# Spreading the twelve gates over the partitions: from TensorE and ScalarE to the DMA queue of GpSimd

## The chip, the core and the metric

One NeuronCore of a Trainium2 chip runs the whole program in one launch. The metric is the device time in microseconds (us), the median of three runs. Engine names are those of the profile: PE is TensorE's matrix multiplication, PEld its weight loads, DVE is VectorE, ACT is ScalarE, POOL is GpSimd, SP the engine that issues most of the DMAs. A name with a q (SPq, POOLq) is the engine's own instruction queue.

## The reference, cut to what matters

Four sequences (b) of 1024 rows and 256 columns go through a transformer block and then through a second cross attention. In the block, nine modulation vectors of 256 numbers are computed for each sequence, and three of them are **gates**: they multiply what the self attention, the cross attention and the MLP give back before it is added to x.

```
m = silu(mod) @ w_ada + b_ada                      # per sequence: 9 x 256
sh_msa, sc_msa, g_msa, sh_mca, sc_mca, g_mca, sh_mlp, sc_mlp, g_mlp = ...
h = _self_attn(_ln(x) * (1 + sc_msa) + sh_msa, w_qkv, b_qkv, w_so, b_so)
x = x + h * g_msa
h = _topk_cross_attn(..., w_co, b_co);   x = x + h * g_mca
h = _swiglu(..., w_m1, b_m1, w_m2, b_m2); x = x + h * g_mlp
# then the second cross attention, without gates
```

Each of the three branches ends in a product with a weight and the addition of a bias row, so h * g is the same as a product with a weight whose columns were multiplied by the gate, plus a bias row multiplied by the gate. That is how the kernel applies gates: it multiplies w_so, w_co and w_m2, and the rows b_so, b_co and b_m2, once for each of the four sequences.

## The kernel before, in words

Rows are worked on in 16 units of 256 rows (b = sequence, part = quarter of it). Every unit goes through five stages: self attention, selection (the sixteen largest of 77 scores), cross attention, MLP and last attention. All is float32, apart from a few small tiles.

**Order.** Nothing runs in the order in which the source is written. Every operation is handed to a planner (`Plan`, line 222) with an engine, an expected cost, buffers and a priority. `place` (line 311) simulates the engines with these costs, picks buffers from rings, and makes one list; `issue` (line 368) then calls the operations' functions in that list's order. An engine executes its own instructions strictly in that order, and semaphores do the rest. So a function that issues no instruction still takes its place, its cost and its buffers in the plan.

**Gates.** `mod_gate(i)` (line 721, three calls, each for all four sequences) multiplies the activated condition with a chunk of w_ada on PE (line 727) and adds the bias on DVE (line 730); the result is `gates`, a tile of 4 partitions (one for each sequence) by 3 by 256. For the multiplication a gate is needed on all 128 partitions. `gated(b)` (line 1292) does that for sequence b and each of its three gates, called here g0 to g11 with number 3b + i:

- PE, line 1303: a product of a column of the identity, repeated over 128 columns, with the gate's row; this puts the row on all partitions of one of the two PSUM banks of the ring `mm`.
- ACT, line 1306: copies it from PSUM to a tile `gate` of 128 x 256. There are two such tiles (line 861), used in turn.
- POOL, line 1308: bias row times gate; and POOL, line 1310: weight times gate. After both, the `gate` tile is free again.

The weight and the row come by DMAs from SP (`load`, line 589). By the order of times in the trace the two `gate` tiles serve g0, g2, g4, g6, g7, g8 and g1, g3, g5, g9, g10, g11: g5 is held until its weight w_m2 is multiplied late.

**Names used later.** L755: ACT writes the modulated context, out of PSUM. L970 and L973: transposes of small tiles on PE and their copy on ACT. L1098, L1104: the second pass of self attention scores on PE, both needed by the exponential L1108 on ACT; L1116: its weighted sum. L1075: values, L938: projections with a 256 x 256 weight, L1035: output projections, L1247 and L1275: the MLP, L1212: weighted sums of cross attention, all on PE. L919: transposes of the normalized rows. L902, L905, L912: statistics and normalization on DVE, with L907 and L909 (POOL) in their middle. L996: the maximum over scores on DVE. L1011 and L1023: the additions and products of the softmax normalization on POOL. L1049: POOL adds a bias row to x. L1079: DVE adds the values' bias. L1335: idle products that keep PE active. On POOL all these share one queue with L1308 and L1310.

Two buffers decide much of PE's order: `mm` has two PSUM banks, and the scores' `s` has one.

Of the kernel before, what the change touches and what calls it, by code (L numbers as in the profile page):

```python
# [9 lines left out]
F32 = mybir.dt.float32  # L10
BF16 = mybir.dt.bfloat16
AF = mybir.ActivationFunctionType
ALU = mybir.AluOpType
# [3 lines left out]
P = 128  # L17
# [371 lines left out]
def tile_block(ctx: ExitStack, tc: tile.TileContext, a: dict, out: bass.AP):  # L389
    nc = tc.nc  # L390

    x_d, cond_d, ctx_d = a["x"], a["cond_1024"], a["ctx_1024"]
    B, L, C = x_d.shape
# [16 lines left out]
    def ctile(shape, name, dt=F32):  # L410
        return const.tile(shape, dt, tag=name, name=name)
# [7 lines left out]
    ident = ctile([P, P], "ident")  # L419
# [25 lines left out]
    for i in range(3):  # L445
        t = ctile([P, TU, 4, 32], f"parts{i}", BF16)
# [5 lines left out]
    for i in range(2):  # L452
        t = ctile([P, TU, H // 2, VP], f"v_self{i}")
# [3 lines left out]
    pl = Plan()  # L457


    def f_pe(cols, n):  # L460
        return n * (cols * 0.00175 + 0.0095) + 0.1

    def f_act(n):
        return 0.21 + 0.00081 * n

    def f_dve(n):
        return 0.155 + 0.00104 * n

    def f_pool(n):
        return 0.13 + 0.00222 * n  # L470
# [7 lines left out]
    T_GATE = ("D", "D", 0.22, 0.05, 0.37, 0.216)  # L478
# [11 lines left out]
    def fixed(name, shape, dt=F32):  # L490
        return pl.fixed(ctile(shape, name, dt), name)
# [8 lines left out]
    n_mod = 26  # L500
    mod = fixed("mod", [P, n_mod, B])
    gates = fixed("gates", [B, 3, C])
    k_ctx = [fixed(f"k_{i}", [P, KC, B, 2, LC]) for i in range(2)]
    v_ctx = [fixed(f"v_{i}", [LC, B, H // 2, VP]) for i in range(2)]
    for v, fill in zip(v_ctx, (0.0, 1.0)):
# [7 lines left out]
    start, total = {}, 0  # L513
# [52 lines left out]
    bg_ada = at.buf("bg_ada", [B, 3, C])  # L566
# [22 lines left out]
    def load(buf, src, kb, prio, key=None, eng="SP", view=None):  # L589
        def fn():  # L590
            dst = buf() if view is None else view(buf())
            (nc.sync if eng == "SP" else nc.scalar).dma_start(dst, src)
        pl.op(eng, f_dma(kb) if eng == "SP" else 0.3, fn, w=[buf if key is None else (buf, key)],
              prio=prio, lag=2.0)
# [21 lines left out]
    for g, names in enumerate(groups):  # L616
        for name, hi in names:
            n, r = hi // P, n_rows[g]
# [11 lines left out]
    def chunk(name, lo, n, prio):  # L630
        c = pl.buf("chunk", f"{name}{lo}")
        load(c, a[name].rearrange("(kc p) n -> p kc n", p=P)[:, :, lo : lo + n], n, prio,
             view=lambda t: t[:, :, :n])
        early.append((chunk_lo, chunk_hi, c))
        return c
# [49 lines left out]
        nc.scalar.preload_act_table_set("natural_log_exp_and_others")  # L685
    pl.op("ACT", 1.5, silu, w=[sc_t], r=[pc], prio=-50, lag=-1.28)

    turn = [0]

    def mod_group(name, lo, m, scale_first, prio, dma_prio):  # L690
# [30 lines left out]
    def mod_gate(i, prio, dma_prio):  # L721
        c = chunk("L0_xcond_w_ada", (3 * i + 2) * C, C, dma_prio)
        pp = pl.buf("mm", f"modg{i}")

        def fn():
            for kc in range(KC):
                nc.tensor.matmul(pp()[:B, :C], sc_t()[:, kc, :B], c()[:, kc, :C],
                                 start=(kc == 0), stop=(kc == KC - 1))
        pl.op("PE", f_pe(C, 2), fn, w=[pp], r=[sc_t, c], prio=prio)
        pl.op("DVE", f_dve(256), lambda: nc.vector.tensor_tensor(  # L730
            gates()[:, i, :], pp()[:B, :C], bg_ada()[:, i, :], ALU.add), w=[(gates, i)], r=[pp, (bg_ada, i)], prio=prio)

    def filled(v):

# [55 lines left out]
    for i, key in enumerate("kqv"):  # L790
        weight(w_qkv, "L0_xcond_w_qkv", -84 + i, (1, 0, 2)[i] * C, C, key)
    mod_gate(0, -30, -79)
    mod_group("L0_xcond_w_ada", 3 * C, 6, False, -3, -70)
    load(cx, ctx_d.rearrange("b k c -> k b c"), 308, -69)
    weight(w_kv[0], "L0_xcond_w_kv", -68)
    weight(w_q0, "L0_xcond_w_q", -67)
    mod_gate(1, -2, -59)
    mod_group("L0_xcond_w_ada", 6 * C, 12, False, -1, -50)
    mod_gate(2, -1, -49)
    mod_group("L1_xcond_Wss_q", 0, 18, True, -1, -48)  # L800
    mod_group("L1_xcond_Wss_kv", 0, 22, True, -1, -47)
# [9 lines left out]
    for b in range(B):  # L811
        pl.op("DVE", 0.42, lambda b=b: nc.vector.bn_stats(st_c()[:LC, b, :], cx()[:, b, :]),
              w=[(st_c, b)], r=[cx], prio=-1)
    for b in range(B):
        pl.op("DVE", 0.16, lambda b=b: nc.vector.bn_aggr(mv_c()[:LC, b, :], st_c()[:LC, b, :]),
              w=[(mv_c, b)], r=[(st_c, b)], prio=-1)
# [475 lines left out]
    def gated(b, pr):  # L1292

        gw = {}
        for i, (key, name, kc) in enumerate(
            (("so", "L0_xcond_w_so", KC), ("co", "L0_xcond_w_co", KC), ("m2", "L0_xcond_w_m2", NF))
        ):
            first = None if b else DMA_FIRST[i]
            w, row = pl.buf("w_" + key, f"w_{key}{b}"), pl.buf("row", f"b_{key}{b}")
            gate, pg = pl.buf("gate", f"gate{b}{i}"), pl.buf("mm", f"pg{b}{i}")  # L1300
            load(w, a[name].rearrange("(kc p) n -> p kc n", p=P), 128 * kc, first or pr)
            load(row, a[f"L0_xcond_b_{key}"].partition_broadcast(P), 128, first or pr)
            pl.op("PE:gate", T_GATE, lambda i=i, pg=pg: nc.tensor.matmul(
                pg()[:, :C], ident[:B, b : b + 1].to_broadcast([B, P]), gates()[:, i, :], start=True, stop=True),
                w=[pg], r=[(gates, i)], prio=pr, take=[gate])
            pl.op("ACT:gate", f_act(256), lambda gate=gate, pg=pg: nc.scalar.copy(gate(), pg()[:, :C]),
                  w=[gate], r=[pg], prio=pr)
            pl.op("POOL:gate", f_pool(256), lambda row=row, gate=gate: nc.gpsimd.tensor_tensor(  # L1308
                row(), row(), gate(), ALU.mult), w=[row], r=[row, gate], prio=pr)
            pl.op("POOL:gate", f_pool(256 * kc), lambda w=w, gate=gate, kc=kc: nc.gpsimd.tensor_tensor(  # L1310
                w(), w(), gate().unsqueeze(1).to_broadcast([P, kc, C]), ALU.mult),
                w=[w], r=[w, gate], prio=pr)
            gw["b_" + key], gw["w_" + key] = row, w
        return gw

    stages = (self_attention, selection, cross_attention, mlp, last_attention)
    for b in range(B):
        pl.at = None
        gw = gated(b, b * NU - 0.5)
        for part in range(NU):  # L1320
            u = Unit()
            u.b, u.part, u.name = b, part, f"_{b}{part}"
            u.prio = float(b * NU + part)
            pl.at = None
            u.x = pl.buf("x", "x" + u.name)
            move_x(u, x_d, False)
            for k, stage in enumerate(stages):
                pl.at = (b * NU + part, k)
                u.prio = ORDER[b * NU + part][k]
                stage(u, gw)  # L1330
# [45 lines left out]
```

## Time and profile before

| | us |
|---|---|
| runs of the kernel (three) | 1040.08, 1040.41, 1044.87 |
| median | 1040.41 |
| the profiled execution | 1041.43 |
| its span, first to last instruction | 1039.4 |
| one core's granted TensorE clock, mean | 0.993 |

The profiled execution's time is 2.0 us more than its span, and 1.0 us more than the median of the runs. The page shows busy times of engines over the span, forty slices of it, the chain of work that ended last (followed back from the end by what released each instruction), and groups of instructions. For forty slices of 26 us:

```profile
PE   7899999999999999999999999999999999999997
...
DVE  5177999979899999947833446599999977724232
ACT  3358786687687794758468667877688765764665
POOL 3384445466353573557635647546335464753653
PEclk9799999999999999999999999999999999999999
DMA  7710000001000000100000200000000001000000
```

A digit is the busy share of a slice in tenths. DMA is busy only in the first two slices. The clock row's 7 is the one stretch with a lower granted clock, from 35.1 to 48.8 us of the span, where it was 0.5. PE is at 9 nearly everywhere, but busy includes waits between overlapping instructions.

### The profile page before, as it was taken

The page shows a single profiled execution, that of the slowest core. Times are in us where ns is not written, and L with a number is a line of the kernel's source. Part 1 is how long each engine was busy: PE and PEld are TensorE (multiplying, and loading weights), DVE is VectorE, ACT ScalarE, POOL GpSimd, SP SyncE. Part 2 cuts the span into 40 slices and gives each one's busy share as a digit, 9 for nine tenths or more (in the row PEclk, how much of TensorE's full clock was granted, in tenths as well). Part 3 has the DMA queues.
Part 4 walks back from the last instruction along what each step waited for, and adds up shares of the span by engine and source line. Part 5 has one row for each costly group of instructions (what it writes and reads, how often), then busy time and mean ns, then how long its engine had stood idle before and what let it go on. Part 6 is the DMA issues. An engine that isn't in the chain of part 4 may idle for free.

```text
span 1039.4 us, 27476 instructions
## 1 busy us (share of the span) xinstructions
PE 1012.0 (97%) x10363; PEld 770.5 (74%) x10363; DVE 757.3 (73%) x4000; ACT 723.5 (70%) x1270; POOL 542.1 (52%) x751
## 2 busy tenths in 40 slices
PE   7899999999999999999999999999999999999997
PEld 5667777777777778777877777778767787778775
DVE  5177999979899999947833446599999977724232
ACT  3358786687687794758468667877688765764665
POOL 3384445466353573557635647546335464753653
PEclk9799999999999999999999999999999999999999
DMA  7710000001000000100000200000000001000000
GB/s 255 242 50 7 3 2 1 3 3 36 3 22 27 7 3 5 38 16 22 21 1 2 82 22 21 2 2 2 2 2 22 2 2 42 12 1 12 2 21 21
DMA packets 23623, 27.01 MB, mean 26 GB/s; under 512 B 1609, under 2 KB 20675, under 8 KB 23491
## 3 DMA queue, kind: packets, MB, share of 16 engines
q1 hardware_dynamic: 23455, 25.26, 7.7%
q8 instruction: 81, 1.33, 0.5%
q14 instruction: 52, 0.42, 0.1%
q10 hardware_dynamic: 35, 0.01, 0.0%
HBM read 21.07 MB, written 4.19 MB: 24 GB/s over the span
## 4 chain that ended last, share of the span: by engine, by line
PE 48%; DVE 13%; ACT 6%; POOL 2%; issue 1%; POOLq 0%; ACTq 0%; DVEq 0%
PE mm L1247 13%; PE mm L1275 8%; PE mm L938 5%; PE mm L1035 5%; PE s L1196 4%; PE o L1212 3%; PE s L985 3%; DVE share L1153 2%; DVE r L1147 2%; DVE nm L996 2%; PE s L1186 1%; DVE share L1145 1%; DVE share L1151 1%; PE mm L919 1%; ACT prob L1108 1%
## 5 line engine op out<-in xcount | busy, mean ns | idle before, releaser
L1247 PE MATMUL mm<-share,w_m 128*128 128x256 f32 x640 | 150.3, 386 | 0.4 <-ACT share L926 0.2
L1205 ACT ACTIVATE prob<-s 77x2048 f32<-77x2048 f32 x64 | 120.0, 1875 | 43.7 <-PE s L1201 43.4
L996 DVE TENSOR_REDUCE nm<-s 128x16 f32<-128x2048 f32 (+1 forms) x64 | 119.0, 1859 | 38.0 <-PE s L985 17.2
L1247 PEld LDWEIGHTS mm<-share,w_m 128*128 128x128 f32 x640 | 117.7, 190 | 26.0 <-issue 4.7
L1147 DVE MATCH_REPLACE8 r<-share 128x77 f32<-128x77 f32 x512 | 109.9, 222 | 0.0
L1145 DVE MAX8 share<-share 128x8 f32<-128x77 f32 x512 | 94.4, 225 | 21.0 <-ACT share L1138 21.0
L1153 DVE MATCH_REPLACE8 share<-share,r 128x77 f32<-128x77 f32 x512 | 109.6, 221 | 0.0
L1011 POOL TENSOR_TENSOR share<-share 128x256 f32<-128x256 f32 x64 | 47.1, 736 | 96.4 <-ACT share L1008 95.1
L1151 DVE MAX8 share<-r 128x8 f32<-128x77 f32 x512 | 93.9, 224 | 0.0
L1247 PE MATMUL mm<-slab,w_m 128*128 128x256 f32 x384 | 92.9, 388 | 0.7 <-ACT slab L926 0.5
L1023 POOL TENSOR_TENSOR slab<-slab,share 128x256 f32<-128x256 f32 x96 | 69.4, 730 | 28.4 <-ACT share L1018 19.2
L1261 POOL TENSOR_SCALAR slab<-slab 128x512 f32<-128x512 f32 x43 | 64.4, 1498 | 36.8 <-ACT slab L1259 33.0
L1247 PEld LDWEIGHTS mm<-slab,w_m 128*128 128x128 f32 x384 | 69.9, 190 | 15.6 <-issue 3.1
L1275 PE MATMUL mm<-share,slab 128*128 128x256 f32 x344 | 80.9, 381 | 0.0
L1008 ACT ACTIVATE share<-o,mask 128x256 f32<-128x256 f32 x128 | 66.6, 575 | 12.2 <-PE o L1212 9.6
L1108 ACT ACTIVATE prob<-s 128x2048 f32<-128x2048 f32 x32 | 60.5, 1889 | 17.9 <-PE s L1104 17.5
L1044 DVE TENSOR_TENSOR slab<-slab,mm 128x512 f32<-128x512 f32 x52 | 35.4, 680 | 50.9 <-PE mm L1035 25.7
L1275 PEld LDWEIGHTS mm<-share,slab 128*128 128x128 f32 x344 | 64.7, 190 | 10.0 <-issue 0.9
L1253 ACT ACTIVATE slab<-mm,cols 128x256 f32<-128x256 f32 x90 | 43.0, 480 | 41.0 <-PE mm L1247 40.5
L1212 PE MATMUL o<-prob,v 77*32 77x256 f32 x1024 | 67.9, 385 | 0.8 <-ACT share L1018 0.5
L1049 POOL TENSOR_TENSOR slab<-slab,row 128x512 f32<-128x512 f32 x39 | 49.9, 1278 | 28.5 <-DVE slab L912 15.4
L907 POOL TENSOR_SCALAR rs<-mv 128x2 f32<-128x2 f32 x64 | 14.2, 222 | 81.7 <-DVE mv L905 78.8
(183 smaller groups left out, 2427.0 us busy)
## 6 DMA issues: line engine op xcount, KB each, us to landing
share<-in_L_xcond_w_m_dram SPq DMA_DIRECT2D x4, 1024.0 KB
slab<-in_x_dram SPq DMA_DIRECT2D x9, 256.0 KB, 2.9
out_dram<-slab SPq DMA_DIRECT2D x9, 256.0 KB, 2.7
w_m<-in_L_xcond_w_m_dram SPq DMA_DIRECT2D x4, 512.0 KB, 6.8
share<-in_L_xcond_w_ada_dram SPq DMA_DIRECT2D x3, 512.0 KB, 3.8
w_so<-in_L_xcond_w_so_dram SPq DMA_DIRECT2D x4, 256.0 KB
w_co<-in_L_xcond_w_co_dram SPq DMA_DIRECT2D x4, 256.0 KB, 4.0
w_qkv<-in_L_xcond_w_qkv_dram SPq DMA_DIRECT2D x3, 256.0 KB
```

Source lines behind the costliest of these rows:

```text
L996: pl.op("DVE:max", f_dve(n), lambda: nc.vector.tensor_reduce(nm()[:, t], s4(), AX.X, ALU.max, negate=True), w=[(nm, t)], r=[s], prio=u.prio)
L1008: pl.op("ACT:nln", 0.5, lambda e=e, own=own, other=other: nc.scalar.activation(nz()[:, e, :], o()[:, ts(e, UT)], AF.Ln, bias=own, scale=ot ...
L1023: nc.gpsimd.tensor_tensor(dst, dst, shaped(nz()[:, k, :], dst), op)
L1108: pl.op("ACT:exp", f_act(2048), lambda s=s, prob=prob: nc.scalar.activation(prob(), s(), AF.Exp), w=[prob], r=[s], prio=pr)
L1145: nc.vector.max(top()[:, h + i, 0:8], sc()[:, h + i])
L1147: nc.vector.match_replace(r1()[:, i], top()[:, h + i, 0:8], sc()[:, h + i], NEG)
L1151: nc.vector.max(top()[:, h + i, 8:16], r1()[:, i])
L1153: nc.vector.match_replace(sc()[:, h + i], top()[:, h + i, 8:16], r1()[:, i], NEG)
L1205: pl.op("ACT:exp", f_act(2048), lambda s=s, prob=prob: nc.scalar.activation(prob()[:LC], s()[:LC], AF.Exp), w=[prob], r=[s], prio=pr)
L1212: nc.tensor.matmul(o()[r, :UT] if drops is not None else o()[r, ts(e, UT)], columns(v_z()[:, b], 8 * c + 2 * j + e), prob()[:LC, j, ts(e, ...
L1247: nc.tensor.matmul(pp()[:, ts(half, UT)], w_m1()[:, kc, m : m + P], ht()[:, kc, :], start=(kc == 0), stop=(kc == KC - 1))
L1275: nc.tensor.matmul(pp()[:, ts(t, C)], gts[f // 2]()[:, f % 2, ts(t, P)], w_m2()[:, f, :], start=(f == 0), stop=(f == NF - 1))
```

## The change

A tensor `gates_d[i]` of 4 x 256 in the outer memory is added for each of the three gate kinds.

- In `mod_gate`, after the DVE addition, POOL's queue stores the finished `gates` row block to `gates_d[i]`; for the first two kinds the same function at once issues the read of the first gate into its tile (g0 and g1).
- `read_gate(n, place)` finds the next gate from number n on that uses the tile `place`, and issues, on POOL's queue, a DMA that reads its 256 numbers from the outer memory into all 128 partitions (1 KB to each, 128 KB written).
- In `gated`, PE's product and ACT's copy issue nothing any more, but they keep their place, cost and PSUM bank in the plan, so all other operations keep their order and their buffers.
- POOL's two multiplications stay. After the second of them, whichever comes second, `read_gate` is called for the next gate of the same tile.

```diff
+    dram = ctx.enter_context(tc.tile_pool(name="dram", bufs=1, space=bass.MemoryType.DRAM))
+    gates_d = [dram.tile([B, C], F32, tag=f"gates_d{i}", name=f"gates_d{i}") for i in range(3)]
...
+    gate_of = {}
+
+    def read_gate(n, place):
+        todo = [m for m in range(n, 3 * B) if gate_of[m]() is place]
+        if todo:
+            b, i = divmod(todo[0], 3)
+            nc.gpsimd.dma_start(place, gates_d[i][b, :].partition_broadcast(P))
...
-        pl.op("DVE", f_dve(256), lambda: nc.vector.tensor_tensor(
-            gates()[:, i, :], pp()[:B, :C], bg_ada()[:, i, :], ALU.add), w=[(gates, i)], r=[pp, (bg_ada, i)], prio=prio)
+        def add():
+            nc.vector.tensor_tensor(gates()[:, i, :], pp()[:B, :C], bg_ada()[:, i, :], ALU.add)
+            nc.gpsimd.dma_start(gates_d[i], gates()[:, i, :])
+            if i < 2:
+                read_gate(i, gate_of[i]())
+        pl.op("DVE", f_dve(256), add, w=[(gates, i)], r=[pp, (bg_ada, i)], prio=prio)
...
-            pl.op("PE:gate", T_GATE, lambda i=i, pg=pg: nc.tensor.matmul(
-                pg()[:, :C], ident[:B, b : b + 1].to_broadcast([B, P]), gates()[:, i, :], start=True, stop=True),
-                w=[pg], r=[(gates, i)], prio=pr, take=[gate])
-            pl.op("ACT:gate", f_act(256), lambda gate=gate, pg=pg: nc.scalar.copy(gate(), pg()[:, :C]),
-                  w=[gate], r=[pg], prio=pr)
+            gate_of[3 * b + i] = gate
+            pl.op("PE:gate", T_GATE, lambda: None, w=[pg], r=[(gates, i)], prio=pr, take=[gate])
+            pl.op("ACT:gate", f_act(256), lambda: None, w=[gate], r=[pg], prio=pr)
+            uses = []
+
+            def times_gate(t, g, n=3 * b + i, gate=gate, uses=uses):
+                nc.gpsimd.tensor_tensor(t, t, g, ALU.mult)
+                uses.append(t)
+                if len(uses) == 2:
+                    read_gate(n + 1, gate())
```

The two POOL operations of a gate then call `times_gate` with the row and with the weight, in place of the two multiplications written out there before.

## The prediction

> **What bounds the kernel now.** I read the busy shares first, then the chain of work that ended last, then, by windows, the chain and the timeline around each of the twelve gates.
>
> ```profile
> PE 1012.0 (97%) x10363; PEld 770.5 (74%) x10363; DVE 757.3 (73%) x4000; ACT 723.5 (70%) x1270; POOL 542.1 (52%) x751
> PE 48%; DVE 13%; ACT 6%; POOL 2%; issue 1%; POOLq 0%; ACTq 0%; DVEq 0%
> ```
>
> PE looks full, but carries only 48% of the span on the chain. The shares add up to about 70% because the chain can be followed back only to about 310 us. From there it runs on DVE up to 341 us, on PE for most of the rest, on DVE again about 500 to 514 us, and on POOL and ACT about 542 to 565 us. Before 310 us I use the busy times: DVE is busy 57.5 of 60 us in 120 to 180 and 55.9 in 240 to 300, so DVE nearly fills that stage too. A PE step is worth its time only where PE is on the chain.
>
> **What goes, and its price.** The sources of the three steps:
>
> ```profile
> L1303 PE MATMUL mm<-gates,ident x24: 372/454/791, 34.5 to 563.7; 4*128 4x256 f32 x24
> L1306 ACT COPY gate<-mm x12: 354/372/530, 35.2 to 567.4; 128x256 f32<-128x256 f32 x12
>   ACT gate L1306: 22.4, 6
> ```
>
> Twelve gates make 24 matmul records and 12 ACT copies of 0.37 us. The last line is of L1308, POOL's row product: POOL stood idle 22.4 us, six times, until a copy. That looks like the prize, but nothing is listed as waiting for L1308 or L1310, so it is idle time of an engine that is seldom the bound. In the stream a gate takes 0.52 to 0.63 us of PE, from its start to the next group's (336.08 to 336.61 for g8, 563.40 to 564.02 for g11). The copies save 12 x 0.37 = 4.5 us of ACT, which has 30% idle.
>
> **The start, to 60 us.** The half clock is granted here, and PE is what the others wait for (DVE waits 12.7 us for L1075).
>
> ```profile
> 37.28 1.22 PE L1303 MATMUL mm<-gates,ident 4*128 4x256 f32 x2 [0.89 <-ACT share L755]
> ...
> 38.97 0.81 PE L1098 MATMUL s<-slab,k_eo 32*128 32x128 f32 x6
> ...
> 42.11 1.16 PE L1303 MATMUL mm<-gates,ident 4*128 4x256 f32 x2
> 43.20 1.22 PE L1075 MATMUL mm<-w_qkv,slab 128*128 128x256 f32 x2
> ```
>
> g3 holds PE from 42.11 to 43.20: 1.09 us. g2 runs mixed into L1098: from L1098's first start to that of L1104 it is 2.45 us, against 1.87 for the next such pair at the same clock (46.91 to 48.78): 0.58. L755, whose last part frees the bank for L970, starts at 35.89 behind g0's slot and copy; without them about 0.5 earlier. Gain before L1075: 1.09 + 0.58 + 0.5 = **2.2 us**.
>
> Against it stand the new transfers. g0 to g3 are read before 60 us, 4 x 128 KB = 0.52 MB, in a stage where DMA moves 302 GB/s (36 to 48 us, share 0.90): loads behind them land up to 1.7 us later, and the last x loads land at 58.3. Their end is not the only thing waited for, so I take half: +0.9; bounds 0 and 1.7.
>
> The stores and first reads stand in POOL's queue between L909 (ends 8.3) and L821 (20.7), and between L965 (ends 24.1) and g0's product (35.6): holes of 12.4 and 11.5 us. In the second, POOL waits for the addition of gate 1 (ends 29.8), then for its store to land, then for gate 2's addition (31.4). A store of x lands 1.9 to 3.2 us after its issue in this trace; under load a 128 KB row took 6.7. Two issues plus 3 us from 29.8 reach about 35, still no later than 35.6; with 6.7 us, g0's product comes 3 us late, and the 4.56 us for which POOL is idle before L1011 (52.09) swallow that. If all this cover were gone, it would cost those 3 us.
>
> **What a POOL-issued DMA costs.** No row of before shows one. Nearest below is SP's issue of the same shape (a 128 KB row at 69.17): 0.35 us of its queue. The Trainium skill, "DMA: Bandwidth & Descriptors", Specifications, gives about 1 us to the first byte on the GpSimd path against about 0.6 on the SP path. But a rule speaks against the change: "SBUF — State Buffer", section "SBUF: two separate sides", says that GpSimd cannot write a DMA's descriptors while DVE holds their shared port pair, with 620 ns growing to 3100. DVE is busy 96% where g4 to g8 fall, though mostly in operations with two inputs or reductions, while the rule is about copies and operations with a scalar; the nearest candidate, L912, lasts 0.4 us. No run here shows the lock. By the first the price p of an issue is 1.0 us, by the second 3.1. I take **p = 1.0** with ends 0.35 and 3.1. Landing: SP's row of 69.17 had its packets moved by about 71.2, so 2 us.
>
> **Where p lands on the path.** Ten reads follow a second product; the page's question is what stands next on POOL. The tight one is behind g3's weight:
>
> ```profile
> 58.11 1.28 POOL L1310 TENSOR_TENSOR w_so<-w_so,gate 128x512 f32<-128x512 f32 x1
> ...
> 59.34 3.02 POOL L1023 TENSOR_TENSOR slab<-slab,share 128x256 f32<-128x256 f32 x4
> ...
> 62.75 0.71 POOL L909 TENSOR_TENSOR rs<-rs,mhalf 128x2 f32<-128x2 f32 x1
> 63.50 0.73 DVE L912 TENSOR_SCALAR slab<-slab,mv,rs 128x256 f32<-128x256 f32 x2 [0.77 <-POOL rs L909]
> ```
>
> POOL runs without a break from 55.4 into these, and DVE then sits idle 0.77 us for L909: +1.0. The start's sum is −2.2 + 0.9 + 1.0 = **−0.3**.
>
> In the DVE stage, 60 to 341 us, the PE slots of g4 to g8 (5 x 0.58 = 2.9) count nothing, since DVE is late next; bounds −2.9 and 0. Reads: behind 96.62 there is a chain of two operations, with idle 0.22 and then 1.78, so nothing at p = 1; behind 237.87 idle is 0.55, so +0.45, halved to +0.2 since L1049 there is followed by ACT work that is not DVE's. Behind g7 (335.23) g8 is read and needed at once: 1.0 + 2.0 us to land, 0.72 for the product, 338.95, where L961 now starts at 338.93: 0. That is the only place where the round trip replaces a PE and ACT path of the same length. The 2.59 us that POOL waited at 118.71 and the 6.26 at 107.77 go; what follows waits for DVE. Sum **+0.2**.
>
> After 341 us, the chain decides:
>
> ```profile
> 507.62 1.37 DVE nm L996
> ...
> 526.87 1.00 PE o L1212 x16
> 527.88 0.62 PE mm L1303 x2
> 528.50 0.59 PE mm L919 x4
> ...
> 562.76 1.76 ACT prob L1205
> ```
>
> g9 (507.29) lies beside DVE's maximum, g11 (563.40) beside ACT's exponential; g10 is itself a link, and 0.62 us go. Of 4.5 us of copies none is a link. Reads behind 424.32 (6.45 us idle), 510.43 (0.29, then 4.02) and 532.83 (1.49, and 8.49 of gate wait gone before it) are hidden; a price of 1 us without that cover would be 3 us. Sum **−0.6**.
>
> Total: −0.3 + 0.2 − 0.6 = −0.7 us. The profiled 1041.43 becomes 1040.7; that execution is 1.0 above the median of the runs, so on the runs' scale **1039.7**.
>
> **Rivals.**
> 1. *Every freed PE step counts* (PE is 97% busy, and the longer links are all PE's): 2.2 at the start and 8 x 0.58 = 4.6 in the stream, POOL's issues and the transfers hidden: −6.8, so 1033.6. Against it: DVE is on the chain or nearly full beside six of the eight.
> 2. *POOL becomes the late one* (slower). With p = 3: 3.0 behind g3's weight, 2.45 behind 237.87, 3 − 2.0 = 1.0 behind 96.62, 2.1 at g8; 8.5, less 2.2 − 0.9 and 0.6 of gains, +6.6: 1047. It decides from p of about 2.6, where four costs less the gains pass 5.2 us. For it: the descriptor rule and a DVE at 96%; against: the DVE operations there are mostly not the kind it names.
> 3. *The start slips.* All 1.7 us of transfer count, POOL's store wait too, and the clock, granted 0.5 for 13.65 us after PE's light stretch at 32 to 34 us, comes back later, since PE has still less to do at 34.5: each 3 us more of it cost about 1.5. Together +3: 1043.4.
> A fourth, that the gates aren't prefetched at all, is excluded but for g8: the other tiles come free many us ahead of use (g10: 510.4 against 530.9).
>
> **How the numbers follow.** Chances: forecast 0.50, first rival 0.17, second 0.23, third 0.10. What can be told from no change is 0.5%, 5.2 us: below 1035.2 or above 1045.6. Faster is the first rival, 0.17; slower the second and a third of the third's tail, 0.26; the rest 0.57. The range takes in most of both rivals: 1034 to 1047. The likeliest case alone, with 0 to 1.7 for the transfers and p from 0.35 to 1.5, is 1037.5 to 1041.5.
>
> **What would show it.** L1303 and L1306 are gone from the profile; L1075's first start is about 41 instead of 43.20; POOL shows 15 DMA issues, whose length is p; DVE's wait for L909 at 63 us is not under 0.77; in the chain L1212 is followed directly by L919 near 527. The forecast is wrong if an issue takes over 2.6 us, if DVE's instructions near the reads become longer, if the half-clock stretch changes in length, or if PE's freed slots in 60 to 341 us appear as an earlier end of that stage.

## The result, and the profile after

The changed kernel takes 1046.52 us in the median (1045.70 to 1048.57) against 1040.41 (1039.27 to 1044.87), nine runs of each. The ratio is 1.0057, interval 1.0044 to 1.007: 0.57% slower, just beyond the 0.5% that the forecast took for what can be told from no change. Its profiled execution took 1046.52 us with a span of 1044.6: 5.1 us more than the span before. In two experiments below (the first four gates by PE; the small DMA) the profiled execution has a spell of half clock between 289 and 298 us, worth 3.2 us, that no other trace here has; these two are read only up to 285 us.

The rows of the page that answer to those shown of before (busy time; the clock over forty slices; the chain that ended last), with the row of the new DMAs (size, median us from issue to landing):

```profile
PE 1004.2 (96%) x10339; PEld 766.0 (73%) x10339; DVE 759.9 (73%) x4000; ACT 720.1 (69%) x1258; POOL 552.6 (53%) x766
...
PEclk9889999999999999999999999999999999999999
...
PE 58%; DVE 24%; ACT 8%; POOL 5%; issue 2%; DMA 2%; POOLq 0%; ACTq 0%; DVEq 0%
...
gate<-gates_d POOLq DMA_DIRECT2D x12, 128.0 KB, 3.3
```

The removal did what it says: 24 matmul records and 12 copies are gone, PE is busy 7.8 us less and ACT 3.4. POOL has 15 instructions and 10.5 us more. The chain now has DMA in it, which before it had not.

**Where the time went** is found with one comparison: each DVE instruction of one trace is put beside the same instruction of the other, and its **lag** is how much later it starts, counted from each span's start. All lags in this document are against the profiled execution of the kernel before. In the changed kernel the lag is 0 up to 36 us, −3.4 at 47, +2.9 from 66 to 240, +5.0 at 300, +4.2 at 320, +5.9 from 380 to 500, and +5.1 from 545 to the end. So the terms are: the start **+2.9**, a jump at 243 us **+2.2**, a chance gain of −0.8 at 303 (a DVE subtraction that before met POOL there and took 1.49 us does not meet it now), a step at 343 us **+1.7**, and a gain at 500 to 530 us **−0.85**; the sum is the 5.1. (Line numbers have moved: L1308 and L1310 are both L1328 now, L912 is L930, L909 is L927, L1011 is L1029, L1023 is L1041, L1049 is L1067, L1158 is L1176, L1075 is L1093, L1212 is L1230, L919 is L937. L746 is a store, L699 a read. L785 and L798 are PE's products for the keys and the values of the context, L801 is DVE's addition behind the latter. In the kernels of the experiments the numbers differ by up to four from these, or from those of before.)

*The start.* Before, the product with w_m2 and L1011 stood so on POOL (start, us, what, and in brackets the idle time before it and what ended it):

```profile
42.34 4.51 POOL L1310 TENSOR_TENSOR share<-share,gate 128x2048 f32<-128x2048 f32 x1 [0.18 <-DMA share<-in_L_xcond_w_m_dram]
...
52.09 0.73 POOL L1011 TENSOR_TENSOR share<-share 128x256 f32<-128x256 f32 x1 [4.56 <-ACT share L1008]
```

In the changed kernel POOL's part of the timeline is this:

```profile
35.41 0.58 POOL L699 DMA_DIRECT2D gate<-gates_d  x1 [4.66 <-DMA gates_d<-gates]
35.98 0.53 POOL L746 DMA_DIRECT2D gates_d<-gates  x1
36.52 0.74 POOL L1328 TENSOR_TENSOR row<-row,gate 128x256 f32<-128x256 f32 x1
37.21 1.27 POOL L1328 TENSOR_TENSOR w_so<-w_so,gate 128x512 f32<-128x512 f32 x1
42.67 0.60 POOL L699 DMA_DIRECT2D gate<-gates_d  x1 [4.19 <-DMA gates_d<-gates]
...
48.70 4.53 POOL L1328 TENSOR_TENSOR share<-share,gate 128x2048 f32<-128x2048 f32 x1 [1.27 <-PE mm L785]
53.20 0.72 POOL L1328 TENSOR_TENSOR row<-row,gate 128x256 f32<-128x256 f32 x1
...
54.81 0.74 POOL L1029 TENSOR_TENSOR share<-share 128x256 f32<-128x256 f32 x1
```

Read it as a queue. The addition of gate kind 2 was done at 31.4, but its store stands behind the read of g1, which waits until 35.4 for store 1 to land (issued at 30.16); so store 2 leaves at 35.98, lands at 42.14, and the read of g2 stands before g1's products until then. That read lands at 48.58, so the product with w_m2 (42.34 before) starts at 48.70; the releaser named in its bracket is not the last one. L1029 comes at 54.81 instead of 52.09. The end of that chain, in windows (busy us of each engine, then granted clock, DMA share, GB/s), and DVE's and PE's instructions:

```profile
51.00:54.00 3.00, 0.99 (x5) 0.41 (x3) 0.00 (x0) 1.14 (x4) 2.91 (x2) 1.00 0.85 269
54.00:57.00 3.00, 0.00 (x0) 0.00 (x0) 0.29 (x1) 0.42 (x1) 2.60 (x5) 0.86 0.57 147
57.00:60.00 3.00, 1.78 (x7) 1.43 (x8) 2.90 (x11) 1.04 (x3) 2.44 (x4) 0.50 0.01 3
60.00:63.00 3.00, 3.00 (x9) 2.25 (x8) 0.89 (x4) 0.40 (x1) 2.60 (x4) 0.51 0.05 14
```

```profile
56.71 1.13 DVE L930 TENSOR_SCALAR slab<-slab,mv,rs 128x256 f32<-128x256 f32 x2 [5.93 <-POOL rs L927]
```

```profile
58.22 1.11 PE L937 MATMUL mm<-ident,slab 128*128 128x128 f32 x4 [6.23 <-DVE v L801]
```

PE has nothing to do from 52 to 58 us, since DVE waits 5.93 us for a small operation in POOL's queue. What doesn't need POOL still ran 4.2 us ahead of the kernel before up to there; the lag of this normalization is +1.8. And then the clock is half from about 56.1 to 63: a second half-clock stretch that the kernel before doesn't have. The first one became shorter, from about 35.7 to 42.5 us instead of from 35.1 to 48.8. The length of the second stretch does not decide the lag: it is 6.8 us in this trace and in those of "g7's read by SP" and "g8 by PE" below, which lag 2.9, 3.0 and 2.2 us at 80 us, and 3.4 us in "g7 by PE" and "small first reads", which lag 3.0 and 2.5.

*243 us.* POOL, and then the one DVE instruction that runs beside it:

```profile
241.00 0.65 POOL L699 DMA_DIRECT2D gate<-gates_d  x1 [0.30 <-POOL w_so L1328]
241.68 1.28 POOL L1067 TENSOR_TENSOR slab<-slab,row 128x512 f32<-128x512 f32 x1
242.92 0.72 POOL L1041 TENSOR_TENSOR slab<-slab,share 128x256 f32<-128x256 f32 x1
243.61 0.72 POOL L1029 TENSOR_TENSOR share<-share 128x256 f32<-128x256 f32 x1
...
245.67 0.72 POOL L1041 TENSOR_TENSOR slab<-slab,share 128x256 f32<-128x256 f32 x1
```

```profile
243.08 3.59 DVE L1176 TENSOR_TENSOR share<-share 128x256 f32<-128x256 f32 x1
```

A subtraction that takes 0.416 us in the median of its 32 took 3.59: it ends when POOL's fifth operation in a row ends, not after the first. Before, it took 0.41:

```profile
240.26 0.41 DVE L1158 TENSOR_TENSOR share<-share 128x256 f32<-128x256 f32 x1
```

*343 us.* The read of g8 and the first product that needs it:

```profile
340.41 0.66 POOL L699 DMA_DIRECT2D gate<-gates_d  x1 [0.30 <-POOL w_co L1328]
343.77 0.72 POOL L1328 TENSOR_TENSOR row<-row,gate 128x256 f32<-128x256 f32 x1 [2.71 <-DMA gate<-gates_d]
344.45 0.20 POOL L979 CAST parts<-nm 128x32 bf16<-128x32 f32 x1
```

The cast that follows (L961 before, at 338.93) came 0.96 us after the row's product then; now it stands directly behind it, 5.5 us later than before.

*500 to 530 us.* The gain is made at 509 us, on DVE. Before, a normalization beside g9 met POOL's weight product (POOL had waited 1.60 us for the copy of g9), and the pair took 1.69 us; it stands in the chain that ended last. Now the product comes ahead of it, and the pair takes 0.84. Before, then after:

```profile
508.90 1.69 DVE L912 TENSOR_SCALAR share<-slab,mv,rs 128x256 f32<-128x256 f32 x2
509.06 1.37 POOL L1310 TENSOR_TENSOR w_so<-w_so,gate 128x512 f32<-128x512 f32 x1
```

```profile
513.37 1.27 POOL L1328 TENSOR_TENSOR w_so<-w_so,gate 128x512 f32<-128x512 f32 x1
514.84 0.84 DVE L930 TENSOR_SCALAR share<-slab,mv,rs 128x256 f32<-128x256 f32 x2
```

DVE's lag falls there from 5.95 to 5.11. PE follows with 5.2, and the forecast's link is gone too: L1230 is followed at once by L937, with no product for a gate between them. That brings L937 to 4.6, but the next L1230 is back at 5.06.

```profile
532.03 1.07 PE L1230 MATMUL o<-prob,v 77*32 77x256 f32 x16
533.03 0.66 PE L937 MATMUL mm<-ident,share 128*128 128x128 f32 x4
```

### The profile page after: what moved, and what is told of

The parts are those of the page before. It is cut to its first block, busy times and chain, and to the rows that moved or that the text cites. A ratio compares the mean times of both kernels' runs of the same rounds, so it can differ in the third digit from the quotient of the medians.

```text
span 1044.6 us, 27432 instructions
## 1 busy us (share of the span) xinstructions
PE 1004.2 (96%) x10339; PEld 766.0 (73%) x10339; DVE 759.9 (73%) x4000; ACT 720.1 (69%) x1258; POOL 552.6 (53%) x766
## 3 DMA queue, kind: packets, MB, share of 16 engines
HBM read 22.64 MB, written 4.21 MB: 26 GB/s over the span
## 4 chain that ended last, share of the span: by engine, by line
PE 58%; DVE 24%; ACT 8%; POOL 5%; issue 2%; DMA 2%; POOLq 0%; ACTq 0%; DVEq 0%
PE mm L1265 14%; PE mm L1293 8%; PE mm L956 7%; PE mm L1053 6%; PE s L1003 5%; DVE r L1165 4%; PE s L1214 4%; DVE share L1171 4%; PE o L1230 4%; DVE nm L1014 3%; DVE share L1163 3%; DVE share L1169 3%; PE s L1116 2%; PE mm L1093 2%; PE s L1204 2%
## 5 line engine op out<-in xcount | busy, mean ns | idle before, releaser
L1029 POOL TENSOR_TENSOR share<-share 128x256 f32<-128x256 f32 x64 | 46.9, 733 | 86.3 <-ACT share L1026 81.7
L1041 POOL TENSOR_TENSOR slab<-slab,share 128x256 f32<-128x256 f32 x96 | 69.6, 731 | 38.7 <-ACT share L1036 19.1
L1062 DVE TENSOR_TENSOR slab<-slab,mm 128x512 f32<-128x512 f32 x52 | 35.4, 681 | 50.5 <-PE mm L1053 25.3
L1230 PE MATMUL o<-prob,v 77*32 77x256 f32 x1024 | 67.9, 385 | 1.2 <-ACT prob L1223 0.7
L1067 POOL TENSOR_TENSOR slab<-slab,row 128x512 f32<-128x512 f32 x39 | 49.9, 1279 | 29.8 <-DVE slab L930 16.7
```

Of the source, the lines that this page charges most:

```text
L1041: nc.gpsimd.tensor_tensor(dst, dst, shaped(nz()[:, k, :], dst), op)
L1230: nc.tensor.matmul(o()[r, :UT] if drops is not None else o()[r, ts(e, UT)], columns(v_z()[:, b], 8 * c + 2 * j + e), prob()[:LC, j, ts(e, ...
```

## The experiments

Theory A: POOL's in-order queue waits for landings in the start; at 243 us its run of operations keeps DVE out; at 343 us the round trip is too long. Rivals: each DMA issue costs a like share (B), or the transfers do (C). The results, as lags in us (the step at 243 is the lag after it minus the lag before it; g0 to g11 are the gates, and "by PE" means by PE and ACT as in the kernel before):

| kernel | lag at 80 us | step at 243 | change 320 to 400 | change 500 to 600 | ratio to before, interval |
|---|---|---|---|---|---|
| changed kernel | 2.9 | +2.2 | +1.7 | −0.85 | 1.0057 (1.0044 to 1.007) |
| first four by PE | 1.2 | +2.1 | not read | not read | 1.0036 (1.0023 to 1.0049) |
| stores ahead | 0.7 | +2.1 | +1.65 | −0.9 | 1.0030 (1.0015 to 1.0046) |
| no spread | −4.0 | 0 | +0.45 | −0.9 | 0.9959 (0.9944 to 0.9975) |
| before, delayed | −1.2 | 0 | 0 | 0 | 1.0002 (0.9987 to 1.0017) |
| before, delayed less | 0.1 | 0 | 0 | 0 | 1.0010 (0.9999 to 1.0022) |
| g7 by PE | 3.0 | 0 | +2.6 | −0.85 | 1.0041 (1.0029 to 1.0054) |
| g0, g1, g7, g8 by PE | −1.0 | 0 | 0 | −0.9 | 0.9993 (0.9986 to 1.0001) |
| g8 by PE | 2.2 | +2.1 | +0.4 | −0.9 | 1.0044 (1.0032 to 1.0057) |
| g7's read by SP | 3.0 | 0 | +1.75 | −0.9 | 1.0040 (1.0025 to 1.0055) |
| before, small DMA | −1.2 | +2.1 | not read | not read | 1.0029 (1.0015 to 1.0042) |
| g1, g7, g8 by PE | −1.1 | 0 | 0 | −0.9 | 0.9997 (0.9986 to 1.0008) |
| small first reads | 2.5 | +2.1 | +1.9 | −0.85 | 1.0057 (1.0035 to 1.008) |

How far a lag can be trusted is in the three kernels whose code is that of before up to 238 us: at 80 us they lag −1.2, 0.1 and −1.2. **The start of the same code varies by about 1.2 us**; the profile of before is a late one. The steps at 243 and after 500 repeat to 0.1 us. The chance gain of 0.8 at 303 us comes and goes, in "delayed less" too, so the table leaves 300 to 320 us out. The start of the changed kernel is in four traces (its own, g7 by PE, g8 by PE, g7's read by SP), with lags of 2.2 to 3.0. Ratios that differ by under about 0.0019, or 2 us (an estimate from the widths of the intervals), can't be told apart: where a total below moved by less, the lag in the trace decides.

**1. What the removal alone gives.**

```diff
-            nc.gpsimd.dma_start(gates_d[i], gates()[:, i, :])
-            if i < 2:
-                read_gate(i, gate_of[i]())
+            if i < 2:
+                nc.gpsimd.memset(gate_of[i](), 0.5)
...
-            nc.gpsimd.dma_start(place, gates_d[i][b, :].partition_broadcast(P))
+            pass
```

> No gate is spread: the two gate tiles are filled with 0.5 once at the start, and PE's product, ACT's copy, the stores and the reads are all left out; POOL's multiplications stay. This is what the removal alone gives. By the prediction's own sum 1040.4 - 2.2 - 0.6 = 1037.6 (PE counts only where it is on the chain); by the rival that every PE step counts, 1033.6. Theory A also expects no wait on POOL before 50 us, L1097 no later than 44 us, and a lag at 60 us of about -3; what happens at 243 us depends on whether POOL's run of additions again meets the DVE addition L1176: without, -3, with it +2.3 on top.

This kernel leaves the gates out: their tiles hold 0.5. Measured 1037.35 us, with no jump at 243. The start gains 4.0 us against the profile of before, 2.8 against its early executions; that is an upper bound, since POOL's products here wait for no gate at all. Between 80 and 320 us, where the slots of five gates are gone, the lag changes by 0.15 us: PE is not the bound there. At 500 to 530 us 0.9 us are gained. The removal is worth about 4 us, and the changed kernel lost some 10 on top of it.

**2. The start.**

```diff
-            if i < 2:
-                read_gate(i, gate_of[i]())
+            if i != 1:
+                read_gate(i // 2, gate_of[i // 2]())
```

> The changed kernel with one DMA moved in POOL's queue: the store of gate kind 2 goes ahead of the read of g1, so no read of g2 waits for a store that was held behind the read of g1. All DMAs and their bytes stay. Theory A: POOL's wait of 4.19 us at 42 us is gone, the product with w_m2 starts about 44 instead of 48.70, and the lag at 60 us falls from 2.9 to between 0 and 1; total 1044.0. Theory B (price of an issue): unchanged, 1046.5. Theory C (transfers): unchanged, 1046.5, lag at 60 us 2.9.

The lag at 80 us falls from 2.9 to 0.7, as theory A has it, below all four traces with the old order, and the total by 2.8 us by the ratios. No DMA and no byte was taken away. POOL's timeline of this kernel:

```profile
31.98 0.53 POOL L746 DMA_DIRECT2D gates_d<-gates  x1 [0.93 <-DVE gates L745]
35.73 0.58 POOL L699 DMA_DIRECT2D gate<-gates_d  x1 [3.22 <-DMA gates_d<-gates]
...
38.76 0.61 POOL L699 DMA_DIRECT2D gate<-gates_d  x1 [0.48 <-POOL w_so L1328]
42.56 0.72 POOL L1328 TENSOR_TENSOR row<-row,gate 128x256 f32<-128x256 f32 x1 [3.19 <-DMA gate<-gates_d]
```

Store 2 leaves at 31.98, and g2's read follows g0's weight with 0.48 us of idle time instead of 4.19. What is left is the wait for the read of g1, 3.19 us. (The product with w_m2 starts at 46.63; I had expected 44.)

The other rival for the start are the bytes. Here the first four reads bring 1 KB instead of 128 KB (so g0 to g3 are left out on the other 127 partitions, which two fills at the start set to 0.5):

```diff
+            np_ = 1 if todo[0] < 4 else P
-            nc.gpsimd.dma_start(place, gates_d[i][b, :].partition_broadcast(P))
+            nc.gpsimd.dma_start(place[:np_, :], gates_d[i][b, :].partition_broadcast(np_))
```

> The changed kernel with the first four reads cut to one partition (1 KB instead of 128 KB each), the tiles filled with 0.5 beforehand by POOL; so the gates g0 to g3 are left out on 127 partitions. Every DMA keeps its place in POOL's queue and its waits. Theory A (POOL's in-order waits for the stores' landings, 4.96 and 6.16 us, and for the reads'): if landings stay 5 us or more, the lag at 60 to 80 us stays above 2; if the small reads land in 2 to 3 us, part of it goes, but the 4 us wait of g2's read for the third store stays. Theory C (128 KB each delay the loads): the lag at 80 us falls by 1.7 or more, to about 1.

The lag at 80 us stays at 2.5, the ratio is the same 1.0057. The small reads landed in a median of 5.4 us, and the wait of g2's read is still there:

```profile
42.98 0.57 POOL L700 DMA_DIRECT2D gate<-gates_d  x1 [4.24 <-DMA gates_d<-gates]
```

So no cost of the bytes is seen: the 0.4 us are within the scatter of the start. A DMA's time to land, and its place in POOL's queue, are left.

With the first four gates spread as before, and the three stores kept:

```diff
+    BY_PE = (0, 1, 2, 3)
...
+            pl.op("PE:gate", T_GATE, spread if old else lambda: None, ...
```

> The gates g0 to g3 are spread by PE and ACT as in the kernel before; g4 to g11 come by DMA, and the three stores stay. Theory A (POOL's in-order queue waits for landings in the start: +2.9; a DVE addition is held up by POOL at 243 us: +2.3; g8's round trip: +1.1; 0.9 back at 500 to 530): the lag behind the kernel before is under 0.7 us at 60 us, the jump at 240 to 247 us stays if the read is still 0.4 us in POOL's way, total about 1043.6. Theory B (every DMA issued by POOL costs a like share, 5.1 us over 15 of them = 0.34 each): four reads fewer, 1045.1, and a lag at 60 us of about 1.7. Theory C (the transfers themselves delay the loads of x and the clock): as A, 1043.6.

The lag is 0.1 at 60 us and 1.2 at 80; the jump at 243 us is there. The step between is the read behind g3's weight: DVE now waits 1.79 us for POOL, against 0.77 before.

```profile
64.66 0.74 DVE L931 TENSOR_SCALAR slab<-slab,mv,rs 128x256 f32<-128x256 f32 x2 [1.79 <-POOL rs L928]
```

By the ratios 2.2 us are won back; I had expected 2.9. Theory B's 1045.1 is not told apart by the total, but B is out by the experiment with the stores, where nothing but the order changed.

**3. The 243 us.** First, is it the read of g7? g7 alone by PE (the edit of the last diff, with 7 in the tuple):

> The changed kernel with g7 alone spread by PE and ACT, so that POOL issues no read behind g6's weight at 241 us; the read of g8 and all others stay. Theory A: the DVE addition L1176 near 243 us takes under 1 us, the jump of 2.2 us at 243 is gone, and the start's 2.9 and g8's 1.1 stay: 1044.2. Theory B (0.34 us for each DMA issue): 1046.1.

The jump is gone, to 0.01 us, and the subtraction shows no long case there. The total is 1.7 us lower by the ratios; in the trace some is given back between 320 and 400 us, where the lag grows by 2.6 instead of 1.7. This trace has half clock from 344.7 to 348.1 us, which the changed kernel's has not, and most of the 0.9 appears from there on; that it is the cause was not tried.

Next, is it the delay? In the kernel before, fills take the read's place, for two lengths (256 and 227 columns):

```diff
+                if n == 6:
+                    for _ in range(3):
+                        nc.gpsimd.memset(gate()[:, :227], 0.5)
```

> The kernel before, with three fills of the gate tile (about 0.95 us of POOL together) behind the product of g6's weight at 237.9 us, where the changed kernel issues its read of g7. No DMA is added. Theory A (a delay of about 0.4 us lets POOL's run of additions get ahead of the DVE addition L1158, which is then held up for the whole run): that one instruction takes about 3.6 us instead of 0.41, and the lag behind the kernel before is about 2.3 us from 247 us on; total 1042.7. Theory B or C (issue price, or something of the DMA itself): only the delay of 0.4 us, of which nothing is seen at the end: 1040.5.

> The kernel before with the three fills behind g6's weight made shorter (227 columns instead of 256), so that POOL's run of additions starts as late against the DVE addition L1158 as in the changed kernel (0.16 us ahead of it instead of 0.09). Theory A1 (only this alignment decides): the DVE addition takes 3.6 us and the lag behind the kernel before grows by about 2.2 at 243 us; total about 1043. Rival A2 (the read that POOL has just issued is what keeps DVE out; a mere delay does not): it takes under 1 us, and the total stays at the kernel before's, 1040.5 to 1041.

Theory A as I had it is wrong here. DVE's subtraction took 0.92 and 0.88 us (the second is shown): it waited for one POOL operation and got in ahead of the next. The total did not move.

```profile
240.42 0.88 DVE L1158 TENSOR_TENSOR share<-share 128x256 f32<-128x256 f32 x1
```

POOL's run and DVE met nearly as in the changed kernel (POOL's addition began 0.09 and 0.14 us ahead of the subtraction; 0.16 there). A delay gives no jump. Nor is it the fills that let DVE in: in the kernel before, with neither a fill nor a DMA, the same subtraction meets two POOL operations in a row at 204 us and gets in after the first.

```profile
203.57 1.27 POOL L1049 TENSOR_TENSOR slab<-slab,row 128x512 f32<-128x512 f32 x1 [0.99 <-DVE share L912]
204.80 0.91 POOL L1011 TENSOR_TENSOR share<-share 128x256 f32<-128x256 f32 x1
```

```profile
204.10 1.02 DVE L1158 TENSOR_TENSOR share<-share 128x256 f32<-128x256 f32 x1
```

What then is it about the read? Its data, or its issue?

```diff
+            if todo[0] == 7:
+                for _ in range(3):
+                    nc.gpsimd.memset(place[:, :227], 0.5)
-            nc.gpsimd.dma_start(place, ...
+            (nc.sync if todo[0] == 7 else nc.gpsimd).dma_start(place, ...
```

> The changed kernel with the read of g7 issued by SP, at the same point of the order, and three fills of 227 columns of the same gate tile on POOL in the place of its issue. The same 128 KB land at about the same time, and POOL is delayed alike. If data landing in the tile (or traffic) keeps the DVE addition L1176 out at 243 us, it takes 3.6 us and the total is 1046.5; if it is POOL's own issuing of a DMA (theory A2), it takes under 1 us, the jump at 243 us is gone, and the total is about 1044.3, as with g7 by PE.

```diff
+                if n == 6:
+                    nc.gpsimd.dma_start(gate()[:1, :], a["L0_xcond_b_so"].partition_broadcast(1))
```

> The kernel before with one small DMA issued by POOL (one row of 1 KB into one partition of the free gate tile) behind g6's weight at 237.9 us; PE and ACT still spread all gates. If a DMA issue on POOL alone is what lets POOL's run keep DVE out (theory A2), the DVE addition L1158 takes 3.6 us and the lag grows by 2.2 to 2.5 us at 243 us: about 1043. If it takes the 128 descriptors or the 128 KB of the broadcast, it takes under 1 us and the total is 1040.5 to 1041. Theory A1 (alignment alone) needs the same delay of about 0.4 us and would give 3.6 us if the start of POOL's addition falls 0.16 us ahead of it.

The same 128 KB issued by SP at 241.91: the subtraction takes 0.87 us, no jump.

```profile
243.23 0.87 DVE L1179 TENSOR_TENSOR share<-share 128x256 f32<-128x256 f32 x1
```

The kernel before with one DMA of 1 KB issued by POOL, POOL first and then DVE:

```profile
236.98 0.76 POOL L1314 DMA_DIRECT2D gate<-in_L_xcond_b_so_dram  x1 [0.30 <-POOL w_so L1312]
237.76 1.30 POOL L1049 TENSOR_TENSOR slab<-slab,row 128x512 f32<-128x512 f32 x1
239.00 0.74 POOL L1023 TENSOR_TENSOR slab<-slab,share 128x256 f32<-128x256 f32 x1
239.68 0.73 POOL L1011 TENSOR_TENSOR share<-share 128x256 f32<-128x256 f32 x1
...
241.73 0.72 POOL L1023 TENSOR_TENSOR slab<-slab,share 128x256 f32<-128x256 f32 x1
```

```profile
239.07 3.67 DVE L1158 TENSOR_TENSOR share<-share 128x256 f32<-128x256 f32 x1
```

3.67 us, and a step of 2.1 us, with POOL 0.08 us ahead: the meeting at which, after fills, DVE got in. This DMA landed 1.9 us after its issue, so before the two met. The issue of a DMA by POOL is what makes the difference, not its bytes, its landing or the delay. Over all traces: with the DMA just ahead (the changed kernel, first four by PE, stores ahead, g8 by PE, small first reads, small DMA) the subtraction is passed over at four boundaries of POOL's operations, six times out of six; without it (before and seven variants of it or of the changed kernel), never. Three of these eight met as closely (the two delays, the read by SP); in the other five the subtraction began 0.6 us into POOL's first operation and was not held at all.

**4. The round trip of g8**, spread by PE instead:

> The changed kernel with g8 alone spread by PE and ACT: no round trip behind g7's weight. Theory A: POOL's wait of 2.7 us for the landing at 343 us is gone, and the step of about 1.1 us there with it (it may be up to 0.6 less, since PE's product is back): 1045.4 to 1046. Theory B (a like share of each DMA): 1046.2. What tells: the lag behind the kernel before grows by under 0.4 us between 320 and 360 us instead of by 1.3.

The lag grows by 0.40 between 320 and 360 us instead of 1.34, as expected, and with no gate spread at all it grows by 0.5 too: by the lag from 320 to 400 us, g8's read accounts for about 1.3 of the 1.7. From the start of the product with w_co to the row's product it takes 4.94 us (338.83 to 343.77), against 3.12 with PE and ACT (338.73 to 341.85).

**5. A version that keeps what pays.** g0, g1, g7 and g8 by PE and ACT, the others by DMA; and one with g0 by DMA too:

> g0, g1, g7 and g8 are spread by PE and ACT, the other eight come by DMA, so no read is issued ahead of g0's product, none at 241 us and none where it is needed at once. Theory A: of the start's PE gain about 1.7 us (the slots of g2 and g3) is kept, since POOL's read of g2 behind g0's weight waits at most 1 us for its store, and the product with w_m2 that comes 2 to 3 us late is covered by POOL's idle 4.56 us before L1011; nothing at 243 and 343 us; 0.9 us less at 500 to 530. Total about 1038.5. Theory B (0.34 for each of 11 DMAs, less the gains): 1041 to 1044.

> As the version with g0, g1, g7 and g8 by PE, but g0 too comes by DMA: its store and its read stand in the hole of POOL's queue before 20.7 us, so no wait is added behind 24 us. Theory A: one slot of PE less at 34 us, 0.3 to 0.6 us off the start; total 1039.5 to 1040.2, ratio to the kernel before about 0.9988. Theory B: 0.34 more, 1040.7.

All three losses are gone: 1.0 us ahead at 80 us, nothing at 243 and 343, 2.0 ahead at the end by the traces. But the start of before is itself 1.2 us earlier in other executions, so only the 0.9 us at 500 to 530 are sure, and the medians (1040.40 against 1040.83, and 1040.95 against 1041.04) can't be told from no change. My 1038.5 was too low by the start's gain.

## Why the prediction was wrong, by its steps

The forecast was 1039.7, no change; the profiled execution came out at 1046.52, near the upper end of the range. The second rival's 1047 is near it by luck: it rests on an issue price of 3 us, and the issues took 0.53 to 0.76.

- **The start, −0.3: measured +2.9. This is the step that failed most.** The gain of 2.2 before L1075 was there, and more (L1093 first starts at 40.81, as the 41 of the forecast). The read behind g3's weight takes 0.64 us of issue and 0.30 of waiting, 0.94 against p = 1.0. That was luck: the 1.0 was taken from a time to the first byte, which is not the time for which an issue holds its queue. It costs its 1.0 us only where nothing else is late (the first four gates by PE); in the changed kernel DVE does not wait there. The bytes were put at 0.9, and no cost of theirs is seen. What failed is the sentence that POOL's idle time before L1011 would "swallow" a late g0. I had followed one landing (store 1) and stopped; the queue holds a second store behind the first read, and a second read behind that store, each of which lands in 5 to 6.5 us in this stage. Landing added to landing gives 6.4 us at the product with w_m2, more than the 4.56 us of cover.
- I had written that the forecast is wrong if the half-clock stretch changes in length. It did, twice: the first became some 7 us shorter, and the idle PE brought a second one of about as much. The third rival had the start's sum, +3.0, with 1.7 of it for bytes whose cost is not seen; its number is luck too. The clock became 0.5 some 4.1 us after PE had run dry at 52.0; the Trainium skill ("TensorE: Matmul & The Clock Gate", "What's actually happening") has it fall to half after an idle window of about 3.4 us.
- **60 to 341 us: +0.2, measured +2.2 at 243.** The reading of POOL's timeline was right to the tenth: idle 0.55, and 0.44 us of delay. The halved cost was wrong, since what counted was not who waits for L1049, but which DVE operation runs beside POOL's. I had brought the rule on ports in for the DMA's descriptors; the section next to the one I used (the Trainium skill, "SBUF — State Buffer", "Who interferes with whom") says that a DVE instruction with two SBUF inputs contends with a POOL instruction that reads SBUF. That fits the ordinary cases of 0.87 to 0.92 us. The page has the later instruction blocked for as long as the earlier one lasts; 3.59 us over five POOL operations is beyond that, and no row of before shows such a case.
- The PE slots of g4 to g8 count nothing: right, 0.15 us over 240 us of program with no gate spread.
- **g8, 0: measured about +1.3.** The path was right, the term too short. From the end of w_co's product to the end of the row's I had 3.72 us (1.0 + 2.0 + 0.72) and no slack; measured are 4.38 (340.11 to 344.49). I had read a landing of 2 us off an SP row; one issued by POOL takes 3.28 here, its issue of 0.66 included. The other half of the 1.3 I had not seen: the product itself starts 4.87 us later than before, where DVE lags 4.21, because it starts 3.40 us after the load of w_co is issued instead of 2.74. With no gate spread it is 3.39, so it isn't the round trip; why the load is used later stays open.
- **After 341 us, −0.6 for g10: measured −0.85**, and the nearness is luck. PE's link went as foreseen, but the lag that lasts to the end is the one gained at 509 us, beside g9, which I had counted as nothing. There I had asked only whether PE or ACT was on the chain, and not that POOL's product, freed from its wait for the copy, would no longer meet DVE. The traces show this; no run isolates it.

## What to carry to other kernels

When DMAs are put into the queue of an engine that also computes, write out that queue in order, with every landing as a wait, and add the landings along it; each DMA behind a waiting one inherits its wait. Taking the products and copies away was worth 4 us here and only at two places, in one of them because POOL no longer waited for a copy; the new waits came where cover was assumed from a single idle time. And a POOL-issued DMA ahead of an unbroken run of POOL operations can shut DVE out for the whole run, so issue it from SP, as was tried here, or put it where POOL is idle afterwards, which was not tried.

## What the runs showed of the hardware that was not expected

- After a DMA issued by POOL, an unbroken run of POOL's two-input operations kept a two-input DVE operation out for 3.57 to 3.67 us, past four boundaries; without the DMA the same operation got in at the first boundary, 0.87 to 1.02 us. That the issue is the cause is shown by the DMA of 1 KB against fills and against the SP issue, all at one place of one program; why POOL then does not give way is open, and so is how long it lasts: in these traces POOL ran without idle time from the issue to the end of the hold.
- Counted from the issue, DMAs of 128 KB issued by POOL landed in 3.3 us when little else moved, and one of 1 KB in 1.9; in the start those of 1 KB took 3.7 to 6.3 us.
